# Cross-attention and experts in one kernel: the first blocks' tables in two sub-blocks instead of three, and two values products one chunk later

## The chip, the cores and the metric

The kernel runs on one core of a Trainium2 chip. The metric is the device time of one execution in microseconds (us); three runs of the kernel before gave 897.76, 898.35 and 902.75, median 898.35. The engines have names in the profile: PE is TensorE's matrix multiplication and PEld its weight load, DVE is VectorE, ACT is ScalarE, POOL is GpSimd, and SP is the engine that issues most of the transfers; SPq is its queue.

## The reference

A token matrix x (4 x 1024 tokens of 256 numbers) attends to a context of 77 rows per batch with 16 heads of 64. What comes out is added to x, and each token then goes through two of nine experts (gated feed-forward networks, 256 to 704 and back), whose sum is added again. Cut to what matters:

```
q = layernorm(layernorm(x)) @ Wq;  k, v = split(layernorm(ctx) @ Wkv)      # q scaled and shifted per head
x = x + softmax(q k^T / 8) v @ Wout
logits = layernorm(x) @ Wr;  top 2 of softmax(logits), weights made to sum to 1
x = x + sum over the two experts e:  w_e * ( silu(y Wg[e]) * (y Wu[e]) ) @ Wd[e],   y = layernorm(x)
```

## The kernel before

The keys are folded into the query weights and the output weights into the values, so that attention over a piece of tokens is: scores against a table `g`, a softmax, and a product with a table `u`. The 4096 tokens are eight groups (`NG`) of 512, each of four sub-blocks of 128 tokens: 32 sub-blocks (`N_SUB`). One loop walks over them, and its body holds work of several sub-blocks at different stages. In its step i:

- `scores(i, k)` and `exponentials(i, k)` (lines 271 to 286) for three banks k: TensorE makes 16 x 77 scores, VectorE the maxima of the rows, ScalarE the exponentials;
- `attention_weights(i - 1)` (lines 306 to 313): VectorE normalises into a single buffer `an`;
- `weights_turn(i - 1)` (lines 327 to 335): VectorE transposes in 32 x 32 pieces into a single buffer `anT`; SP writes it to DRAM (`a_d`, 640 KB) and reads it back turned, in four transfers, into `aT` (two buffers). The next transpose must wait until `a_d` is written, the four reads too;
- `values(d)` with d = i - 3 (line 344): TensorE multiplies `aT` by `u`; `attended(d)` (lines 352, 353) adds the product to x and to the router's logits;
- pieces of the routing of groups whose attention is done: `residual` writes x to the output (line 861), `normalised` makes the layer norm y and writes it to `y_d` (line 896), `choices` picks the two experts (lines 903 to 938), `places` gives each token its place in its experts' lists and scatters eight columns of entries there with GpSimd's indirect transfers (line 965). In `choices`, GpSimd makes the token numbers of the entries (lines 932 and 937), and VectorE then writes the weights beside them (line 938). A list of pending work that a generator yields is advanced by `advance(what, n)`: n operations, or all of them.

The experts' work is cut into blocks of 256 or 128 tokens of one expert. Which expert and where its list starts is computed on the chip. For the first six blocks (`EARLY`) this is done when only the first four groups are routed: `early_blocks` is a chain of 20 small VectorE operations after a count by TensorE (lines 984 to 1050). It begins in step 24 of the loop and is advanced by a fixed number of operations in each step. When the chain has ended, `fetch(in_parts=True)` issues for blocks 0 and 1 the list and token gathers on GpSimd's queue (line 1208) and makes generators for the weights, kept in `partly`. From the next step on one part of them is issued per step on SP's queue, behind that step's `a_d` and `aT`: the gate weights (line 1191, 704 KB), the up weights (lines 1193 to 1195, 704 KB in three transfers), the down weights (lines 1197 and 1201, 704 KB in two); a fourth step ends the generator. What is left is issued after the loop. `fetch` stands in the loop's body ahead of the first part of `choices` of the same step.

SP's queue is worked in order: a transfer that waits holds up those behind it. The same holds for each engine's instructions, in the order in which the program writes them; `manual_schedule` leaves that order as written.

After the loop come the blocks. `hidden_pair(j, also)` makes the six chunks of a block's hidden layer (gate and up products, line 1265, then line 1271 on ScalarE and 1272 on VectorE). After each chunk `pump()` advances the pending routing work by up to twelve operations; a yielded `PRODUCT` makes it pause for three chunks (`HOLD`). Then the functions in `also[chunk]` are called. In block 0 these are the values of the last two sub-blocks, whose weights have not come back from DRAM when the loop ends, and the transposition of block 1's tokens, `turn(1)` (line 1251):

```
in_first = {0: [lambda: late_values(N_SUB - 2)], 3: [last_values], 4: [lambda: turn(1)]}
```

`late_values(i)` is `values(i)` and `attended(i)` with the statistics of the sub-block before. `last_values` does this for sub-block 31 and puts the last group's routing and the tables of the later blocks on the list of pending work.

Of the kernel before, what the change touches and what calls it, by code (L numbers as in the profile page):

```python
# [21 lines left out]
def kernel(  # L22
# [222 lines left out]
    def query(i):  # L245

        g, s = divmod(i, NS)
        o, r, _ = zscale[g]
        nc.scalar.activation(
            zs[i % 2][:, : D - 1], xg[g][:, s, : D - 1], AF.Identity,  # L250
            bias=o[:, s : s + 1], scale=r[:, s : s + 1],
        )

    def query_turn(i):
        z = zs[i % 2]
        pz = mm_tile(f"pz{i}")
        for c in range(C):
            nc.tensor.transpose(pz[:, c * P : (c + 1) * P], z[:, c * P : (c + 1) * P], ident)
        zT = zTs[i] = pools["qpool"].tile([P, C, P], F32, tag="zT", name=f"zT{i}")
        nc.scalar.copy(zT.rearrange("p c t -> p (c t)"), pz[:, : C * P])  # L260

    def scores(i, k):

        zT = zTs[i]
        h, n = banks[k]
        if k == 0:
            nmx[i] = stat.tile([P, H], F32, tag="mx", name=f"mx{i}")
        psc = pscs[k] = ps_sc.tile([P, TB], F32, tag=f"sc{k}", name=f"psc{i}_{k}")
        w = n * J + (E if h + n == H else 0)
        for c in range(C):  # L270
            nc.tensor.matmul(  # L271
                psc[:, :w], zT[:, c, :], g_sb[i // NS // GPB][:, c, h * J : h * J + w],
                start=(c == 0), stop=(c == C - 1),
            )
        nc.vector.tensor_reduce(  # L275
            nmx[i][:, h : h + n], psc[:, : n * J].rearrange("p (h j) -> p h j", h=n), AX.X,
            ALU.max, negate=True,
        )

    def exponentials(i, k):  # L280
        h, n = banks[k]
        if k == 0:
            exs[i] = pools["qpool"].tile([P, H, J], F32, tag="ex", name=f"ex{i}")
            sms[i] = stat.tile([P, H], F32, tag="sm", name=f"sm{i}")
        for q in range(n):
            nc.scalar.activation(  # L286
                exs[i][:, h + q, :], pscs[k][:, q * J : (q + 1) * J], AF.Exp,
                bias=nmx[i][:, h + q : h + q + 1], accum_out=sms[i][:, h + q : h + q + 1],
            )
# [12 lines left out]
    def attention_weights(i):  # L302

        ex, sm = exs.pop(i), sms.pop(i)
        rs = stat.tile([P, H], F32, tag="rs", name=f"rs{i}")
        nc.vector.reciprocal(rs, sm)
        an = an_of[0]
        nc.vector.tensor_tensor(  # L308
            an[:, : H * JA].rearrange("p (h j) -> p h j", h=H), ex[:, :, 0:JA],
            rs.unsqueeze(2).to_broadcast([P, H, JA]), ALU.mult,  # L310
        )
        four = H // N2
        nc.vector.tensor_tensor(
            an[:, H * JA :].rearrange("p (m w n) -> p n m w", w=W, n=N2)[:, :, :, :JR],
            ex[:, :, JA:J].rearrange("p (n m) j -> p n m j", n=N2),
            rs.rearrange("p (n m) -> p n m", n=N2).unsqueeze(3).to_broadcast([P, N2, four, JR]),
            ALU.mult,
        )
# [4 lines left out]
    def weights_turn(i):  # L323


        turned = pools["qpool"].tile([P, NQ, Q, KC], F32, tag="anT", name=f"anT{i}", bufs=1)
        nc.vector.transpose(  # L327
            turned.rearrange("p q t k -> p q k t"), an_of[0].rearrange("p (k q t) -> p q k t", q=NQ, t=Q)
        )
        aT = aTs[i] = pools["qpool"].tile([P, NQ, Q * KC], F32, tag="aT", name=f"aT{i}")  # L330
        there = a_d[i % 2]
        nc.sync.dma_start(out=there, in_=turned.rearrange("p q t k -> p (q t k)"))
        by_key = there.rearrange("(a i) (q m) -> q i a m", i=Q, q=NQ)
        for q in range(NQ):
            nc.sync.dma_start(out=aT[q * Q : (q + 1) * Q], in_=by_key[q])
# [28 lines left out]
    with ExitStack() as kvs:  # L364
# [418 lines left out]
        def fill(*what, new=mm_tile):  # L783

            for b, n in what:
                first_keys(b, n, new)
# [96 lines left out]
    def exponential(g):  # L883
        nc.scalar.activation(routed[g]["pb"], routed[g]["pb"], AF.Exp)
# [239 lines left out]
    def of(tiles, j):  # L1124

        return tiles[j % len(tiles)] if j < NBLK else late[id(tiles)]
# [100 lines left out]
    def turned_tile(j):  # L1227
        xT = xTs[j] = late["xT"] if j >= NBLK else pools["spool"].tile(
            [P, C, TS], F32, tag="xT", name=f"xT{j}"
        )  # L1230
        return xT
# [13 lines left out]
    def turn(j):  # L1245

        nh, xT = blocks[j][0], turned_tile(j)
        px = ps_sc.tile([P, TB], F32, tag="sc0", name=f"px{j}").rearrange("p (c t) -> p c t", c=C)
        for c in range(C):
            for h in range(nh):  # L1250
                nc.tensor.transpose(
                    px[:, c, h * P : (h + 1) * P], of(yins, j)[:, h, c * P : (c + 1) * P], ident
                )
        nc.scalar.copy(xT[:, :, : nh * P], px[:, :, : nh * P])  # L1254
# [178 lines left out]
    def advance(what, n=None):  # L1433

        for _ in range(n) if n is not None else iter(int, 1):
            if next(what, None) is None:
                return True
        return False
# [16 lines left out]
    N_SUB = NG * NS  # L1455
    LAG = 3
    chosen, early = None, None
    for i in range(N_SUB + 1):
        g, s = divmod(i, NS)
        now_on = i < N_SUB  # L1460
        d = i - LAG

        gr, sr = divmod(i - LAG + 1, NS)
        q = gr - 1

        if now_on:
            if 0 < i < N_SUB - 1:
                query(i + 1)
            if i:
                scores(i, 0)  # L1470
                fill(*left.get((i, 0), ()))
                exponentials(i, 0)
        if i > 1:
            attention_weights(i - 1)
        if now_on and i:
            scores(i, 1)
            fill(*left.get((i, 1), ()))
            exponentials(i, 1)
        if i > 1:
            weights_turn(i - 1)  # L1480
        if now_on:
            if i:
                scores(i, 2)
                fill(*left.get((i, 2), ()))
            if i == B - 1:
                vsides.close()
            if 0 < i < N_SUB - 1:
                query_turn(i + 1)
            if i:
                exponentials(i, 2)  # L1490
                queries_logits(i)
        else:
            turn(0)
        if d > 0:
            residual_stats(d - 1)
        if gr >= 0 and sr == 1 and q > 0:
            ranks(q - 1)
        if i - LAG + 1 == (G_EARLY + 1) * NS + 2:
            early = early_blocks()
            advance(early, 2)  # L1500
        if d >= 0:
            values(d)

        if s == 0 and 0 < g and g + 1 < NG:
            query_scale(g + 1)
        if s == 1 and g + 2 < NG:
            load_x(g + 2)
        if s == 3 and g + 2 < NG:
            for k in range(NS):
                query_stats(g + 2, k)  # L1510
        if gr >= 0 and sr == 0 and q > 0:
            advance(chosen)
        if gr >= 0 and sr == 1:
            if g + 2 < NG:
                query_variance(g + 2)
            if q >= 0:
                advance(residual(q))
                root(q)
            if g + 2 < NG:
                query_root(g + 2)  # L1520
            nc.scalar.activation(junk, eps_t, AF.Exp)
            if q > 0:
                advance(places(q - 1))
        if gr >= 0 and sr == 2 and q >= 0:
            advance(logits(q))
            exponential(q)
            advance(normalised(q))
        if early is not None:
            if advance(early, 9):
                early = None  # L1530
                now[0] = -1
                fetch(in_parts=True)
        elif partly and advance(partly[0], 1):
            partly.pop(0)
        if gr >= 0 and sr == 3 and q >= 0:
            chosen = choices(q)
            advance(chosen, 14)
        if d >= 0:
            attended(d)
        if i == BH * GPB * NS + LAG - 1:  # L1540
            halves[0].close()
            open_experts()
# [7 lines left out]
    def late_values(i):  # L1550
        residual_stats(i - 1)
        values(i)
        attended(i)
# [6 lines left out]
        rest.append(late_blocks())  # L1560

    rest.append(listed_second_last())
    in_first = {0: [lambda: late_values(N_SUB - 2)], 3: [last_values], 4: [lambda: turn(1)]}


    LAST = NBLK - 1
# [86 lines left out]
```

## Time and profile before

| | |
|---|---|
| median of three runs | 898.35 us |
| the profiled execution | 902.66 us |
| its span, first to last instruction | 900.6 us |
| TensorE busy | 869.1 us, 97% of the span |
| VectorE / ScalarE / GpSimd busy | 592.2 / 356.2 / 312.5 us |
| mean granted TensorE clock | 0.992 |
| attention's loop ends, block 0 begins | about 365 us |

A row of the list in order of time has the start in us from the span's start, the duration, the engine, the line, the operation with what it writes and reads, and how many instructions are merged; in brackets stands how long the engine was idle before, and what ended the idle time. A row of a table by stretches has for PE, PEld, DVE, ACT and POOL the busy time and the number of instructions, then the granted TensorE clock, the busy share of the DMA engines, and what they moved in GB/s. "x20" at line 344 is the ten products of a sub-block, each of which is recorded as two.

### The profile page before, as it was taken

How to read it: one execution, taken by the hardware profiler on the slowest of the kernel's cores; microseconds unless marked ns; L12 is line 12 of the kernel's file. 1: busy time of each engine (PE TensorE's matmuls, PEld its weight loads, DVE VectorE, ACT ScalarE, POOL GpSimd, SP SyncE). 2: the span in 40 equal slices, each digit the busy share in tenths (PEclk: the TensorE clock that was granted, in tenths of full speed). 3: DMA queues.
4: the chain of work that ended last, by engine and by line, in shares of the span. 5: the costliest groups of instructions: out<-in, count | busy, mean ns of one | idle time of the engine just before them, and what ended most of it. 6: DMA issues, size and time to landing. Idle time of an engine off the chain costs nothing. (4 is left out here: it accounts for less than half of the span.)

```text
span 900.6 us, 13822 instructions
## 1 busy us (share of the span) xinstructions
PE 869.1 (97%) x3864; PEld 677.8 (75%) x3864; DVE 592.2 (66%) x1806; ACT 356.2 (40%) x1500; POOL 312.5 (35%) x325
## 2 busy tenths in 40 slices
PE   8999999998999998899999999999999999999996
PEld 6545787866787776788787777777777777778885
DVE  4857788778999978443826666666666656665641
ACT  3668687858788685241121111111111111111110
POOL 3000000404233430537256435435445435445232
PEclk9999999999999999899999999999999999999998
DMA  6116556566766676899579779779779778789722
GB/s 222 49 67 202 152 187 193 113 182 149 216 176 191 188 210 203 213 298 185 158 226 298 218 220 315 223 217 311 224 221 317 219 217 218 226 230 322 217 33 24
DMA packets 132956, 181.18 MB, mean 201 GB/s; under 512 B 26951, under 2 KB 98127, under 8 KB 132752
## 3 DMA queue, kind: packets, MB, share of 16 engines
q1 hardware_dynamic: 115322, 162.90, 60.5%
q0 software_dynamic: 17344, 17.26, 10.3%
q8 instruction: 31, 0.51, 0.3%
q14 instruction: 45, 0.37, 0.1%
q10 hardware_dynamic: 214, 0.13, 0.0%
HBM read 141.54 MB, written 40.39 MB: 202 GB/s over the span
## 5 line engine op out<-in xcount | busy, mean ns | idle before, releaser
L1265 PE MATMUL pg<-xT,wgu 128*128 128x256 f32 x1144 | 253.0, 380 | 3.0 <-DVEq L1606 1.5
L1265 PEld LDWEIGHTS pg<-xT,wgu 128*128 128x128 f32 x1144 | 215.5, 190 | 33.0 <-ACT xT L1254 2.5
L286 ACT ACTIVATE ex<-psc,mx 128x77 f32<-128x77 f32 x512 | 158.7, 331 | 70.3 <-DVE mx L275 66.6
L1343 PE MATMUL po<-wd,hid 128*128 128x256 f32 (+1 forms) x804 | 180.9, 380 | 0.0
L1343 PEld LDWEIGHTS po<-wd,hid 128*128 128x128 f32 (+1 forms) x804 | 149.2, 187 | 28.1 <-issue 3.7
L344 PE MATMUL po<-u,aT 128*128 128x265 f32 x640 | 159.2, 405 | 8.8 <-DMA aT<-a_d 8.8
L344 PEld LDWEIGHTS po<-u,aT 128*128 128x128 f32 x640 | 150.4, 313 | 11.6 <-issue 9.9
L1378 POOL DMA_INDIRECT out_dram<-co,ids x63 | 100.2, 1591 | 167.7 <-DVE co L1346 139.4
L965 POOL DMA_INDIRECT list_d<-r_entry,r_pli x64 | 66.8, 1043 | 260.9 <-DVE r_pli L963 148.1
L1238 DVE STREAM_TRANSPOSE xT<-yin 32x128 f32<-32x128 f32 (+1 forms) x544 | 148.4, 273 | 12.5 <-DMA yin<-y_d,ids 3.7
L271 PE MATMUL psc<-g,zT 128*128 128x462 f32 (+1 forms) x384 | 141.5, 514 | 2.6 <-ACT zT L260 2.6
L1271 ACT ACTIVATE sl<-pg 128x256 f32<-128x256 f32 x130 | 49.7, 384 | 233.8 <-PE pg L1265 162.1
L1272 DVE TENSOR_TENSOR hid<-pg,sl 128x256 f32<-128x256 f32 x130 | 55.0, 424 | 128.9 <-ACT sl L1271 94.7
L271 PEld LDWEIGHTS psc<-g,zT 128*128 128x128 f32 x384 | 71.7, 190 | 61.0 <-issue 46.0
L286 ACT ACTIVATION_READ_ACCUMULATOR ex<-psc,mx 128x1 f32 x512 | 107.9, 211 | 0.0
L327 DVE STREAM_TRANSPOSE anT<-an 128x1280 f32<-128x1280 f32 x32 | 79.6, 2486 | 14.3 <-DMA a_d<-anT 13.8
L1208 POOL DMA_INDIRECT yin<-y_d,ids x67 | 70.5, 1053 | 27.0 <-issue 25.5
L275 DVE TENSOR_REDUCE mx<-psc 128x6 f32<-128x462 f32 (+1 forms) x96 | 53.5, 558 | 18.8 <-PE psc L271 17.7
L1346 DVE TENSOR_SCALAR co<-po,ids 128x256 f32<-128x256 f32 x67 | 32.2, 483 | 48.4 <-PE po L1343 46.8
L308 DVE TENSOR_TENSOR an<-ex,rs 128x1024 f32<-128x1024 f32 x32 | 39.2, 1225 | 1.1
L1331 ACT COPY hid<-ph 128x384 f32<-128x384 f32 x15 | 7.2, 479 | 78.4 <-PE ph L1326 78.4
L1307 ACT ACTIVATE hs<-psg 128x512 f32<-128x512 f32 x15 | 9.0, 597 | 65.3 <-issue 42.2
(311 smaller groups left out, 762.5 us busy)
## 6 DMA issues: line engine op xcount, KB each, us to landing
wgu<-in_L_ffn_Wg_dram SPq DMA_DIRECT2D x41, 704.0 KB
wd<-in_L_ffn_Wd_dram SPq DMA_DIRECT2D x41, 640.0 KB
wgu<-in_L_ffn_Wu_dram SPq DMA_DIRECT2D x41, 512.0 KB
a_d<-anT SPq DMA_DIRECT2D x32, 640.0 KB
aT<-a_d SPq DMA_DIRECT2D x128, 160.0 KB
wgu<-in_L_ffn_Wu_dram SPq DMA_DIRECT2D x41, 128.0 KB
x<-in_x_dram SPq DMA_DIRECT2D x8, 512.0 KB
out_dram<-x SPq DMA_DIRECT2D x8, 512.0 KB
```

What stands on the lines that cost most here:

```text
L271: nc.tensor.matmul(psc[:, :w], zT[:, c, :], g_sb[i // NS // GPB][:, c, h * J : h * J + w], start=(c == 0), stop=(c == C - 1),)
L275: nc.vector.tensor_reduce(nmx[i][:, h : h + n], psc[:, : n * J].rearrange("p (h j) -> p h j", h=n), AX.X, ALU.max, negate=True,)
L286: nc.scalar.activation(exs[i][:, h + q, :], pscs[k][:, q * J : (q + 1) * J], AF.Exp, bias=nmx[i][:, h + q : h + q + 1], accum_out=sms[i][: ...
L327: nc.vector.transpose(turned.rearrange("p q t k -> p q k t"), an_of[0].rearrange("p (k q t) -> p q k t", q=NQ, t=Q))
L344: nc.tensor.matmul(po[:, :DE], aT[:, :, n], u_sb[b][:, n, :], start=(n == 0), stop=(n == KC - 1))
L965: i = nc.gpsimd.indirect_dma_start(out=list_d[:, :], out_offset=bass.IndirectOffsetOnAxis(ap=place_i[:, s : s + 1], axis=0), in_=entries[k ...
L1208: return nc.gpsimd.indirect_dma_start(out=dst, out_offset=None, in_=src, in_offset=bass.IndirectOffsetOnAxis(ap=offsets, axis=0), **kw,)
L1238: yield nc.vector.transpose(xT[q : q + Q].rearrange("p c (h t) -> p h c t", t=P)[:, :nh, :, a : a + Q], of(yins, j)[a : a + Q].rearrange(" ...
L1265: nc.tensor.matmul(pg[:, g, :], w[:, c, at : at + P], xT[:, c, :], start=(c == 0), stop=(c == C - 1),)
L1272: nc.vector.tensor_tensor(hid[:, f, :], pg[:, 1, :], sl, ALU.mult)
L1343: nc.tensor.matmul(po[rows, :D], hid[:, f, at], d[:, f, :], start=(f == 0), stop=(f == NF))
L1378: i = nc.gpsimd.indirect_dma_start(out=out_r, out_offset=bass.IndirectOffsetOnAxis(ap=rows_of(j, h, rows), axis=0), in_=cos[j][:, h, :], i ...
```

## The change

Two lines change. The chain of the first six blocks' tables is advanced by 14 operations per step instead of 9, so that it ends in step 25 instead of step 26, and `fetch` is called one step earlier. And in block 0 the values of sub-block 30 are called after chunk 1 instead of chunk 0, those of sub-block 31 after chunk 4 instead of chunk 3; `turn(1)` stays after chunk 4, behind them.

```diff
         if early is not None:
-            if advance(early, 9):
+            if advance(early, 14):
                 early = None
                 now[0] = -1
                 fetch(in_parts=True)
         elif partly and advance(partly[0], 1):
             partly.pop(0)
...
     rest.append(listed_second_last())
-    in_first = {0: [lambda: late_values(N_SUB - 2)], 3: [last_values], 4: [lambda: turn(1)]}
+    in_first = {1: [lambda: late_values(N_SUB - 2)], 4: [last_values, lambda: turn(1)]}
```

The functions that these lines call are unchanged:

```
    def late_values(i):
        residual_stats(i - 1)
        values(i)
        attended(i)

    def last_values():
        late_values(N_SUB - 1)
        residual_stats(N_SUB - 1)
        rest.append(routing(NG - 1))
        rest.append(late_blocks())
```

The steps in which the weights of blocks 0 and 1 are issued on SP's queue:

| step | before | after |
|---|---|---|
| 26 | | gate 0 |
| 27 | gate 0 | up 0 |
| 28 | up 0 | down 0 |
| 29 | down 0 | |
| 30 | | gate 1 |
| 31 | gate 1 | up 1 |
| 32 | up 1 | down 1 |
| after the loop | down 1 | |

## The prediction

> **What bounds the kernel now.** I began with the page's busy row and the group of the values product (line 344), went to TensorE's list of instructions in order of time for the end of attention, and from its releaser to the SP queue.
>
> ```profile
> PE 869.1 (97%) x3864; PEld 677.8 (75%) x3864; DVE 592.2 (66%) x1806; ACT 356.2 (40%) x1500; POOL 312.5 (35%) x325
> ...
> L344 PE MATMUL po<-u,aT 128*128 128x265 f32 x640 | 159.2, 405 | 8.8 <-DMA aT<-a_d 8.8
> ```
>
> TensorE is the bound: 869.1 of 900.6 us. All that TensorE waits for `aT`, the transposed weights that return through DRAM, is 8.8 us, five waits, and 6.2 us of them are three waits between 349 and 380 us:
>
> ```profile
> 349.74 4.94 PE L344 MATMUL po<-u,aT 128*128 128x265 f32 x20 [0.32 <-DMA aT<-a_d]
> 354.51 0.60 PE L1251 MATMUL px<-ident,yin 128*128 128x128 f32 x4
> 358.69 6.56 PE L344 MATMUL po<-u,aT 128*128 128x265 f32 x20 [3.57 <-DMA aT<-a_d]
> 365.08 1.89 PE L1265 MATMUL pg<-xT,wgu 128*128 128x256 f32 x8
> 366.81 4.86 PE L344 MATMUL po<-u,aT 128*128 128x265 f32 x20
> 371.50 5.34 PE L1265 MATMUL pg<-xT,wgu 128*128 128x256 f32 x24
> 379.16 6.56 PE L344 MATMUL po<-u,aT 128*128 128x265 f32 x20 [2.31 <-DMA aT<-a_d]
> 385.56 1.89 PE L1265 MATMUL pg<-xT,wgu 128*128 128x256 f32 x8
> 387.28 0.60 PE L1251 MATMUL px<-ident,yin 128*128 128x128 f32 x4
> ```
>
> The four L344 rows are the values of sub-blocks 28, 29, 30, 31. A values product takes 4.86 us, but 6.56 after the two long waits: each wait costs its idle time and 1.70 more. From 387.28 us on TensorE runs the experts with no wait for DMA, so what is won or lost before this row is what the kernel wins or loses. The most that can be had here is 3.57 + 2.31 + 0.32 + 2 x 1.70 = 9.6 us.
>
> What `aT` waits for is read from the SP queue (every row is the issue of transfers, in queue order):
>
> ```profile
> 345.37 0.40 SPq L1197 DMA_DIRECT2D wd<-in_L_ffn_Wd_dram  x1
> ...
> 346.63 0.51 SPq L332 DMA_DIRECT2D a_d<-anT  x1
> 353.59 1.74 SPq L335 DMA_DIRECT2D aT<-a_d  x4
> 356.11 0.34 SPq L332 DMA_DIRECT2D a_d<-anT  x1
> 359.89 1.73 SPq L335 DMA_DIRECT2D aT<-a_d  x4
> 361.66 0.43 SPq L861 DMA_DIRECT2D out_dram<-x  x1
> 362.90 0.41 SPq L1191 DMA_DIRECT2D wgu<-in_L_ffn_Wg_dram  x1
> 363.41 0.68 SPq L332 DMA_DIRECT2D a_d<-anT  x1
> 374.08 1.74 SPq L335 DMA_DIRECT2D aT<-a_d  x4
> ```
>
> The loads of `aT` go out when the write of `a_d` has landed. With no weights ahead a write lands in 359.89 - 356.11 = 3.8 us; with an expert's down weights (704 KB) ahead in 353.59 - 346.63 = 7.0; with the output and the gate weights ahead in 374.08 - 363.41 = 10.7. From the issue of `aT` to TensorE's start are 5.1 us (353.59 to 358.69, and 374.08 to 379.16). So the wait of 3.57 us belongs to the down weights ahead of a_d(29), and the wait of 2.31 to what lies ahead of a_d(31).
>
> **Part one: the tables in fewer sub-blocks.** The same 20 small VectorE operations are spread as 14 + 6 instead of 9 + 9 + 2. Nothing is removed. The five that go into sub-block 24 take 0.95 us there (L1011 to L1025, 297.42 to 298.37) and are missing in 25, so `early_ai`, for which GpSimd's gathers wait, is made at the same time (299.0). What moves is `fetch`, one sub-block ahead, and with it every weight load of blocks 0 and 1 on the SP queue: gate weights 0 from sub-block 27 to 26, up 28 to 27, down 29 to 28; gate weights 1 from 31 to 30, up 32 to 31, down from after the loop into 32. I follow the landing of each `a_d` (before in brackets; the row "with the same load ahead" is the measure):
>
> - a_d(26) now has 704 KB ahead: about 321.3 (319.12). Its `aT` is used at 330.94: hidden, and it costs as long as that cover stands nothing.
> - a_d(27): output, up weights, GpSimd's scatters, as many bytes as before, 12.7 us after the one before it as then: 334.0 (331.80).
> - a_d(28): y and down weights instead of y and up weights: 11.5 later, 345.5 (343.35). Its `aT` then comes at 350.6 instead of 349.74; TensorE waits about 1 us there.
> - a_d(29): nothing ahead, but VectorE's transpose waits for a_d(28) and ends at 348.0, plus 3.8: 351.8 (353.59). `aT` at 356.9: the wait of 3.57 becomes about 1.
> - a_d(30): gate weights 1 ahead; about 360.7 (359.89). `aT` some 6 us later, 366.8.
> - a_d(31): output and up weights ahead, where output and gate weights were: the same bytes, the same scatters, 14.2 us after the one before it: 374.7 after taking off 0.2 for scatters begun earlier (374.08).
>
> So the late loads are only passed along: what a_d(29) gains, a_d(31) doesn't keep.
>
> A second step of this part is on GpSimd's queue. `fetch` is called before `choices(4)` instead of after it, so the eight gathers stand ahead of the copies of line 937, and VectorE's line 938 waits for those copies:
>
> ```profile
> 293.73 0.34 POOL L937 COPY r_entry<-r_tg 128x4 int32<-128x4 int32 x2
> ...
> 309.93 0.97 POOL L1208 DMA_INDIRECT ids<-list_d,early_ai  x1 [0.30 <-issue]
> ```
> ```profile
> 309.71 0.42 DVE L938 TENSOR_TENSOR r_entry<-r_m,r_rb 128x4 f32<-128x4 f32 x2
> ```
>
> The gathers end at 310.9, and 0.22 + 0.34 + 0.3 us of small operations bring the copies to 311.5; VectorE would come to line 938 at 310.06 and stands 1.5 us. Behind it are the residual and the row maxima of sub-block 27, and ScalarE's exponentials wait for those. VectorE has 3.2 us idle ahead of 329.19, which takes the stall up; until there TensorE loses 0.4 to 1.0 us on `zT`. This is ahead of the waits above and is swallowed by them as long as the DMA chain sets their ends. I take 0 on the end, with 1.0 us as the price if the cover is gone.
>
> **Part two: values one chunk later.** Sub-block 30's values move from behind chunk 0 to behind chunk 1, 31's from behind chunk 3 to behind chunk 4. No instruction is added or removed. Values 30 are not late today, so that move pays only where part one makes them late: TensorE would be at them at about 363.3 + 1 and waits to 366.8. Values 31 are different: TensorE now waits at 379.16 with chunk 4 still to do (1.72 us, 385.56 to 387.28). Afterwards chunk 4 lies ahead of the wait. The routing of the last group stays where it is, since it is held until the first chunk of block 1 by the product of the second-last group.
>
> The sum has thus one term that counts: gain = 1.72 - d, where d is the delay of a_d(31). With d = 374.7 - 374.08 = 0.6 the turn at 387.28 comes at 386.2: 1.1 us gained. All later work keeps its order. The profiled execution, 902.66 us with a span of 900.6, becomes 901.6; the median of the runs shown, 898.35, lies 4.3 below the profiled execution, and I take the same 1.1 from it: **897.2**.
>
> **A rule against the trace.** The Trainium skill (TensorE: Matmul & The Clock Gate, section on HAM oscillation) says that idle gaps of TensorE matter to its clock above some 3.4 us. By that the new wait of about 3 us ahead of values 31 would leave the clock alone. The trace differs:
>
> ```profile
> 376.00:380.00 4.00, 1.69 (x7) 1.26 (x7) 1.32 (x5) 0.38 (x1) 2.92 (x5) 1.00 1.10 274
> 380.00:384.00 4.00, 4.00 (x12) 3.23 (x12) 0.00 (x0) 0.00 (x0) 0.43 (x1) 0.57 0.92 276
> ```
>
> After 2.31 us idle the granted clock (third number from the end) fell to 0.57 for 3.4 us, worth the 1.70. By the rule the gain would be 1.1 + 1.7 = 2.8 us; I keep the row, 1.1, and both for the range.
>
> **Rivals.**
> - *The DMA chain catches up.* If the 704 KB ahead of a_d(26) are drained while that queue idles (SP shows no write in flight from 319 to 324), nothing is passed along: a_d(28) at 343.3, a_d(29) at 349.5, a_d(30) at 358.8, a_d(31) about 13 later, 371.8. Then the end of values 31 is 381.7 to 383.5: up to 5.6 us gained, 892.8 to 894.6. For it speaks the idle DMA before each landing, against it that a_d(27) and a_d(28) today take 12.7 and 11.5 us each with these bytes.
> - *Nothing is seen.* d is as large as chunk 4: 898.4. The tables' part alone would do that if TensorE's 1 us on `zT` also stays.
> - *Slower, through VectorE's wait at line 938.* If it delays the transposes of sub-blocks 27 to 31 by its 1.5 us each without recovery, a_d(31), 0.6 late already, is up to 5 us late when the up weights' three issues on SP (334.21 to 336.18: 2 us where the gate weights take 0.4) also stand ahead of it. It decides from d = 1.72 on. Price: 2 to 3.5 us, 900.4 to 902.
>
> **Chances.** The forecast (896 to 898.2) 0.48; catching up 0.20; nothing 0.18; slower 0.14. I count changes under 0.5% (4.5 us), about what a measurement of this kernel can tell, as same. Half of the catching up is over 4.5 us gained, with a little for the rule on the clock: faster 0.12. Most of the slower case stays below 4.5 us, but the delay may pass into the experts: slower 0.10. Same 0.78. The range takes in the catching up nearly whole and the slower case to 3 us: 893.2 to 901.4; the forecast's own is 895.5 to 898.9.
>
> **What would show it.** In the changed profile: the wait of values 29 falls from 3.57 to about 1; a new wait ahead of values 30; a longer one, about 3 us, ahead of values 31, with a slow clock after it; the turn at 387.28 at 386.2; VectorE idle about 1.5 us ahead of line 938 with GpSimd as releaser; a_d(26) landing some 2 us later. The prediction is wrong if a_d(31) lands well before 374, if TensorE has a new wait in the experts, or if sub-blocks 26 to 28 get longer.

## The result and the profile after

The changed kernel is slower, by less than half a per cent: median 900.86 us of 20 runs (897.94 to 904.99) against 898.06 of 20 runs of the kernel before (893.27 to 904.10), ratio 1.0044 with a 95% interval of 1.0028 to 1.0059, or some 3.9 us by the ratio. A second comparison (further down) gave 1.0023, 1.0005 to 1.0041. The time lies in the predicted range (893.2 to 901.4), but the sign is wrong: 1.1 us gained was forecast.

Single executions of one kernel lie up to 11 us apart (line 984, ahead of which nothing was changed, begins anywhere from 277.0 to 284.0 us in the profiles here), and the two profiled ones happen to be a slow one of before (902.66) and a fast one of after (898.0). They can't be compared by their spans. What can be compared is the stretch from the count for the tables (line 984 on TensorE: 283.64 us before, 280.69 after) to the turn of block 1's tokens (line 1251: 387.28 and 384.63), since everything that the change touches lies between the two. It takes 103.6 us before and 103.9 after, so this pair of profiles shows hardly any of the 3.9 us; a second pair further down shows 3.2. From that turn to the end are 513.3 us in the first profile of before, which has a lone wait of 1.3 us for `xT` at 437 us, and 511.4 or 511.5 in all thirteen other profiles here, of whatever version: nothing is passed on into the experts.

The page of the changed kernel, the rows of the values product, the scores and VectorE's transpose:

```profile
L344 PE MATMUL po<-u,aT 128*128 128x265 f32 x640 | 157.6, 402 | 4.4 <-DMA aT<-a_d 4.2
...
L271 PE MATMUL psc<-g,zT 128*128 128x462 f32 (+1 forms) x384 | 142.2, 515 | 7.4 <-ACT zT L260 4.6
...
L327 DVE STREAM_TRANSPOSE anT<-an 128x1280 f32<-128x1280 f32 x32 | 79.4, 2483 | 19.4 <-DMA a_d<-anT 19.3
```

TensorE waits less for `aT` ahead of the values (4.2 us, 8.8 before) and more ahead of the scores (7.4, 2.6 before); VectorE's transposes wait longer for `a_d` to be written (19.3, 13.8 before). Some of the waiting has moved from the values into the loop. Where, is seen in TensorE's list in order of time:

```profile
344.67 3.37 PE L271 MATMUL psc<-g,zT 128*128 128x462 f32 x8 [1.09 <-ACT zT L260]
348.59 1.34 PE L271 MATMUL psc<-g,zT 128*128 128x317 f32 x4 [0.55 <-ACT lg L297]
...
350.13 4.94 PE L344 MATMUL po<-u,aT 128*128 128x265 f32 x20
354.91 0.60 PE L1251 MATMUL px<-ident,yin 128*128 128x128 f32 x4
357.05 4.94 PE L344 MATMUL po<-u,aT 128*128 128x265 f32 x20 [1.54 <-DMA aT<-a_d]
361.82 3.62 PE L1265 MATMUL pg<-xT,wgu 128*128 128x256 f32 x16
367.95 6.55 PE L344 MATMUL po<-u,aT 128*128 128x265 f32 x20 [2.52 <-DMA aT<-a_d]
374.34 5.34 PE L1265 MATMUL pg<-xT,wgu 128*128 128x256 f32 x24
379.86 4.93 PE L344 MATMUL po<-u,aT 128*128 128x265 f32 x20 [0.18 <-issue]
384.63 0.60 PE L1251 MATMUL px<-ident,yin 128*128 128x128 f32 x4
```

The wait of values 29 is down from 3.57 to 1.54 us and without the slow clock, as forecast. A new one of 2.52 stands ahead of values 30, with 1.7 us of slow clock. Values 31 hardly wait: TensorE comes to them at 379.7 us, just when their `aT` is due (374.61, below, plus 5.1). They begin 99.2 us after line 984, 95.5 before: 3.65 later, less chunk 4 (1.72) and less the slow clock that is gone there (1.63), leaves 0.3 us lost. SP's queue says why:

```profile
312.35 0.43 SPq L1191 DMA_DIRECT2D wgu<-in_L_ffn_Wg_dram  x1
313.21 0.34 SPq L332 DMA_DIRECT2D a_d<-anT  x1
319.88 3.47 SPq L335 DMA_DIRECT2D aT<-a_d  x4
...
346.77 0.34 SPq L332 DMA_DIRECT2D a_d<-anT  x1
350.67 1.73 SPq L335 DMA_DIRECT2D aT<-a_d  x4
353.21 0.41 SPq L1191 DMA_DIRECT2D wgu<-in_L_ffn_Wg_dram  x1
355.07 0.34 SPq L332 DMA_DIRECT2D a_d<-anT  x1
361.69 1.75 SPq L335 DMA_DIRECT2D aT<-a_d  x4
...
366.09 0.41 SPq L332 DMA_DIRECT2D a_d<-anT  x1
374.61 1.76 SPq L335 DMA_DIRECT2D aT<-a_d  x4
```

The two writes that now have gate weights ahead, a_d(26) and a_d(30), take 6.7 and 6.6 us from issue to landing; a_d(29), which has no weights ahead any more, takes 3.9. Counted from line 984, a_d(30) lands at 81.0 (76.3 before) and a_d(31) at 93.9 (90.4).

The late writes are felt in the loop too. VectorE's transpose of sub-block 28, before and then after:

```profile
332.87 2.50 DVE L327 STREAM_TRANSPOSE anT<-an 128x1280 f32<-128x1280 f32 x1
```
```profile
333.01 2.46 DVE L327 STREAM_TRANSPOSE anT<-an 128x1280 f32<-128x1280 f32 x1 [4.48 <-DMA a_d<-anT]
```

It waits 4.48 us for a_d(27), where it had no wait. VectorE's next reduction of scores (line 275), for which ScalarE's exponentials wait, stands behind it and comes 3.1 us later, counted from line 984.

### The profile page after: what moved, and what is told of

It is laid out like the page before. It is cut to its first block, busy times and chain, and to the rows that moved or that the text cites. A ratio compares the mean times of both kernels' runs of the same rounds, so it can differ in the third digit from the quotient of the medians.

```text
span 896.1 us, 13820 instructions
## 1 busy us (share of the span) xinstructions
PE 866.4 (97%) x3864; PEld 676.3 (75%) x3864; DVE 591.0 (66%) x1806; ACT 356.1 (40%) x1500; POOL 311.6 (35%) x325
## 5 line engine op out<-in xcount | busy, mean ns | idle before, releaser
L327 DVE STREAM_TRANSPOSE anT<-an 128x1280 f32<-128x1280 f32 x32 | 79.4, 2483 | 19.4 <-DMA a_d<-anT 19.3
```

The source lines that it names most:

```text
L327: nc.vector.transpose(turned.rearrange("p q t k -> p q k t"), an_of[0].rearrange("p (k q t) -> p q k t", q=NQ, t=Q))
```

## The experiments

Three theories stood against each other. A: the weights that go out one step earlier delay the chain of `a_d` writes. B: VectorE waits at line 938 for GpSimd's copies behind the gathers. C: the values' move costs. The first four kernels were meant to take the change apart. Each ratio is to the kernel before in the same comparison.

**The tables alone.** The line of the values is put back:

```diff
-    in_first = {1: [lambda: late_values(N_SUB - 2)], 4: [last_values, lambda: turn(1)]}
+    in_first = {0: [lambda: late_values(N_SUB - 2)], 3: [last_values], 4: [lambda: turn(1)]}
```

> Only the tables' half of the change (14 operations per step, fetch one step earlier); the values stay behind chunks 0 and 3. Theory A (the loads of blocks 0 and 1, one step earlier on the SP queue, delay the chain of a_d writes; the values' move only takes chunk 4 out of the way): slower than before by more than the whole change, by about 1.7 us more, so +4 to +6 us; in its trace a_d(31) lands about 3.5 us later, counted from the count of the tables on TensorE (line 984), than in the kernel before. Theory B (VectorE's wait for the token numbers behind the gathers): the same sign, +1.5 to +4. Theory C (the values' move is what costs): no difference, -1 to +1.

Measured: ratio 1.0058 (1.0037 to 1.0078), +5.2 us: more than the whole change, as A says, though the intervals overlap. a_d(31) lands 93.1 us after line 984, 2.6 later than in the first profile of before where 3.5 were expected; values 30 wait 5.61 us.

**The values alone.** The kernel before with the second changed line only.

> Only the values' half (behind chunks 1 and 4); the tables as before. Theory A: faster by chunk 4's 1.7 us, and by up to 1.7 us more where the shorter wait ahead of values 31 spares the slow clock: -1.7 to -3.4 us. Theory B: the same. Theory C: slower by the whole 3 to 4 us.

Measured: 0.9979 (0.9966 to 0.9992), -1.9 us. The move of the values is a gain, as A and B said, and C falls. In its trace values 31 follow chunk 4 with no wait at all.

**The gathers behind the choices' first part.** To put GpSimd's copies ahead of the gathers again, `fetch` is called after the choices of its step:

```diff
                 now[0] = -1
-                fetch(in_parts=True)
+                fetch_due = True
...
             advance(chosen, 14)
+        if fetch_due:
+            fetch_due = False
+            fetch(in_parts=True)
```

> The whole change, but fetch is called after the choices of its step, so that GpSimd's copies of the token numbers stand ahead of the gathers as in the kernel before; SP's queue as in the whole change. Theory A: as slow as the whole change, within 1 us (+2 to +5 against before). Theory B: the loss is gone (-2 to +1), and VectorE's wait at line 938 with it. Theory C: as slow as the whole change.

Measured: 1.0024 (1.0006 to 1.0042), +2.2 us. But this kernel does not do what it was meant to. The first 14 operations of `choices` end before the copies, which are issued in the next step, so the copies still stand behind the gathers. Its last gather and its copies:

```profile
306.85 0.95 POOL L1208 DMA_INDIRECT ids<-list_d,early_ai  x1 [0.30 <-issue]
...
308.15 0.32 POOL L937 COPY r_entry<-r_tg 128x4 int32<-128x4 int32 x2
```

Its time therefore says nothing on B; it is in effect a third measurement of the whole change. The traces do tell. GpSimd and VectorE in the whole change, in order of time:

```profile
308.26 0.32 POOL L937 COPY r_entry<-r_tg 128x4 int32<-128x4 int32 x2
```
```profile
306.90 0.17 DVE L930 TENSOR_TENSOR seen<-r_cums,r_sel 128x9 f32<-128x9 f32 x1
307.11 0.40 DVE L938 TENSOR_TENSOR r_entry<-r_m,r_rb 128x4 f32<-128x4 f32 x2
```

VectorE's line 938 ran at 307.11, before the copies had even begun (308.26). It doesn't wait for them; that they write other columns of the tile may be why. The wait that I had costed at 1.5 us does not exist.

**The weights held back one step.** After `fetch` one step is left empty, so that SP's queue has the order of the kernel before:

```diff
                 fetch(in_parts=True)
+                hold = 1
+        elif partly and hold:
+            hold -= 1
         elif partly and advance(partly[0], 1):
```

> The whole change, but the first part of the weights is held back one step, so that SP's queue has the order of the kernel before; GpSimd's and VectorE's order as in the whole change. Theory A: the loss is gone, and the values' move gains its 1.7 us: -3.4 to 0 against before. Theory B: still slower, +1.5 to +4. Theory C: as slow as the whole change.

Measured: 0.9968 (0.9954 to 0.9983), -2.9 us. With the weights in their old steps the loss is gone, though the gathers still stand ahead of GpSimd's copies as in the changed kernel. That settles A against B.

**Which load?** The next two split the early weights: block 0's early and block 1's as before (an empty step after the last part of block 0: `hold = 1` at the `pop`), and the other way round (block 0 held one step, block 1's first part sent at the `pop`).

> The whole change, but only block 0's weights go out one step earlier; the first part of block 1 stays in step 31 as before (one empty step between). Theory A1 (the loss starts with the gate weights in step 26 and is passed along): still slower, +1 to +4 us against before. Theory A2 (the late landing of a_d(26) to a_d(28) is made good in step 29, which has no load any more, and only gate weights 1 in step 30 delay the last two writes): faster, -5 to -2 us; a_d(30) and a_d(31) land no later after line 984 than in the kernel before (76.3 and 90.4 us).

> The whole change, but block 0's weights stay in steps 27 to 29 as before and only block 1's go out one step earlier (30 to 32). Theory A1: as fast as the values' move alone, -3 to -1 us. Theory A2: the loss is here, +1 to +5 us; four steps in a row with loads, a_d(30) lands 3 us or more later after line 984 than before, and a_d(31) with it.

Measured: block 0 early 1.0019 (1.0004 to 1.0035), +1.7 us; block 1 early 1.0053 (1.0037 to 1.0069), +4.7 us. The greater loss is with block 1's gate weights in step 30, as A2 says, though a_d(30) and a_d(31) land there only 2.8 and 1.1 us later than in the first profile of before, less than A2 expected; and A2's -5 to -2 for block 0 early was missed. Against the values' move alone (-1.9), block 0 early still costs 3.6 us. Its writes 30 and 31 land at 77.5 and 90.5, 1.2 us later than before and as before (76.3 and 90.4), so that part of A2 held for the last write. What differs inside the loop is that VectorE's transpose of sub-block 28 waits 4.84 us for a_d(27) (0.62 in the values' move alone). Its waits of TensorE from 330 to 390 us (in all, how many, the longest):

```profile
PE po L344 <- DMA aT<-a_d: 3.2, 2, 1.9
PE psc L271 <- DVE r_o L916: 1.5, 1, 1.5
PE psc L271 <- ACT zT L260: 1.1, 1, 1.1
PE psc L271 <- ACT lg L297: 0.8, 1, 0.8
```

The last three, 3.4 us, are ahead of the scores; they stand in this stretch of the whole change too (1.1, 1.1 and 0.6), and of the values' move alone they do not. That they come from the late transpose is read from the order of the rows; no run takes it apart. The two costs don't add: 3.6 and 6.6 make 10.2, and the whole change costs 5.8 more than the values' move alone, 4.0 by the second comparison. Why is not shown.

**Fewer loads in the loop.** If the load on the queue is the cause, taking more of it away must gain. First all of block 1's weights go after the loop (parts are advanced in the loop only while two blocks are pending), block 0's staying in steps 27 to 29. Then block 0's down weights too, which are used only after block 1's hidden layer:

```diff
-        elif partly and advance(partly[0], 1):
-            partly.pop(0)
+                hold = 1
+        elif partly and hold:
+            hold -= 1
+        elif partly and issued < 2:
+            issued += 1
+            advance(partly[0], 1)
...
+    advance(partly[1], 2)
     for parts in partly:
         advance(parts)
```

> Weights of block 0 as in the kernel before (steps 27 to 29), all of block 1's after the loop, values moved. By theory A a_d(31) has 704 KB less ahead and lands 2 to 3 us earlier than before (87 to 88 us after line 984); the wait of values 29 stays (2 to 4 us and the slow clock). -5 to -3 us against before, unless block 1 then waits for its weights.

> As the one before, and also block 0's down weights, which are needed only after block 1's hidden layer, go out after the loop, behind block 1's gate and up weights. By theory A values 29 no longer wait behind the down weights: -8 to -4 us against before. If the rule of this stretch were not the load on the queue but VectorE's and ScalarE's own chain, no better than -3.

Measured: block 1 late 0.9973 (0.9954 to 0.9991), -2.4 us: a_d(31) lands 86.4 us after line 984, 4 sooner than before, but this is no better than the weights held (0.9968), so the expected -5 to -3 was missed. Values 31 had no wait left to lose there; values 29 still wait 3.05 us behind the down weights. With those after the loop as well: 0.9942 (0.9920 to 0.9963), **-5.2 us**, median 887.77 of only 7 runs against 893.04. It beats the kernel before, and by that the changed one. TensorE and SP in that version, in order of time:

```profile
353.70 4.86 PE L344 MATMUL po<-u,aT 128*128 128x265 f32 x20
358.39 3.62 PE L1265 MATMUL pg<-xT,wgu 128*128 128x256 f32 x16
361.85 4.75 PE L344 MATMUL po<-u,aT 128*128 128x265 f32 x20
366.44 5.34 PE L1265 MATMUL pg<-xT,wgu 128*128 128x256 f32 x24
372.71 4.93 PE L344 MATMUL po<-u,aT 128*128 128x265 f32 x20 [0.93 <-DVE hid L1272]
377.48 0.60 PE L1251 MATMUL px<-ident,yin 128*128 128x128 f32 x4
```
```profile
352.60 0.34 SPq L332 DMA_DIRECT2D a_d<-anT  x1
355.59 1.74 SPq L335 DMA_DIRECT2D aT<-a_d  x4
357.38 0.43 SPq L861 DMA_DIRECT2D out_dram<-x  x1
359.52 0.34 SPq L332 DMA_DIRECT2D a_d<-anT  x1
365.43 1.74 SPq L335 DMA_DIRECT2D aT<-a_d  x4
```

No wait for `aT` is left; a_d(30) lands in 3.0 us and a_d(31), with only the output ahead, in 5.9. The stretch takes 94.2 us.

**The pair again, and two controls.** The kernel before and the changed kernel once more, for second profiles.

> The kernel before, for a second profile. In the first one 103.64 us lie between the count on TensorE (line 984) and the turn of block 1 (line 1251), and 513.3 us behind it, where every other profile has 511.4 or 511.5. If the first profile was an unlucky execution, this one has about 101 us (the values' move alone has 99.1, and is 1.9 us faster) and 511.4. If not, 103 to 104.

> The whole change, for a second profile. If the stretch between line 984 and the turn of block 1 carries the whole difference of the medians, it has about 104 to 105 us here, 3 to 4 more than the kernel before, and 511.4 us follow it. +3 to +5 us against before.

Measured: before 1.0006 (0.9993 to 1.0019), changed 1.0023 (1.0005 to 1.0041), +2.1 us, a little under what was expected. The stretch takes 103.4 us before and 106.6 after, so this pair shows +3.2. Whether the first profile of before was unlucky in this stretch stays open: 103.4 where 101 was expected speaks against it, but this second profiled execution (898.04) is the slowest of its twenty runs (median 895.62), and the tables held, below, whose queue and values are in the order of before, takes 101.3 in an execution under its median. Block 0 early and block 1 early take 101.3 and 102.0, though their medians lie above that of before. So the sizes of the losses here rest on the times of many runs; a single profile shows where a landing or a wait moved, not by how much the kernel did. What followed the turn in the first profile was unlucky: it is 511.4 here. The later landing of the last write is plainer than in the first pair, 95.7 against 90.1, and so is the wait ahead of values 30 in the changed kernel:

```profile
371.25 6.27 PE L344 MATMUL po<-u,aT 128*128 128x265 f32 x20 [4.26 <-DMA aT<-a_d]
```

Then the fastest version with the values at their old places, and the tables' half with the weights held.

> Down weights of block 0 and all of block 1 after the loop, as in the fastest version so far, but the values of sub-blocks 30 and 31 behind chunks 0 and 3 as in the kernel before. If the values' move pays only where the weights come back late, it is worth nothing here: -6 to -4 us against before, as with the move. If it pays its chunk of 1.7 us anyway: -4 to -2.5.

> Only the tables' half (14 operations per step, gathers ahead of the copies), with the weights held so that SP's queue is as before; values as before. By theory A this does nothing: -1 to +1 us, against +5.2 for the tables' half with the weights one step earlier. If the tables' spread or GpSimd's order costs by itself: +1.5 to +4.

Measured: 0.9961 (0.9948 to 0.9974), -3.5 us, and 1.0015 (0.9992 to 1.0039), +1.3 us. In the first the values' move seems worth its chunk even where `aT` comes back early (-5.2 with it), but the intervals overlap. The second can't be told from no change, nor from the 1.5 us or more of the other theory; the same tables with the weights one step earlier cost 5.2. The weights held (0.9968), which has this spread of the tables too, is no slower than the values' move alone (0.9979), which has not: these runs show no cost of the spread by itself.

The landings over all profiles, in us after line 984 (SP's queue, issue of the `aT` loads):

| | a_d(26) | a_d(30) | a_d(31) |
|---|---|---|---|
| gate 0 in step 26: changed kernel twice, tables alone, gathers behind choices, block 0 early | 38.6 to 39.7 | | |
| gate 0 in step 27: before twice, values alone, held, block 1 early, block 1 late, down 0 late and its old values, tables held | 34.8 to 36.2 | | |
| gate 1 in step 30: changed kernel twice, tables alone, gathers behind choices, block 1 early | | 79.1 to 83.2 | 91.6 to 95.7 |
| gate 1 in step 31: before twice, values alone, held, block 0 early, tables held | | 74.1 to 77.5 | 87.4 to 90.5 |
| block 1 after the loop: three versions | | 72.3 to 74.8 | 82.1 to 86.4 |

Whether a write has the gate weights ahead of it separates the groups: a_d(26), (30) and (31) land at least 2.4, 1.6 and 1.1 us later with them one step earlier. From issue to landing a_d(26) and a_d(30) take 6.0 to 8.2 us in the versions of the first and the third row. All versions send the weights on the same queue as `a_d`, so the runs do not tell whether the order of the queue delays the write or the DMA engines that both share.

## Why the prediction was right or wrong

- *The frame was right in outline only.* The loss is made ahead of block 1's turn, by late landings of `a_d`, and chunk 4 moved ahead of values 31 is a gain (the values alone: -1.9 us). But the sum had one term, the delay d of a_d(31), with a break-even at 1.72 us, and that is too little: block 0 early loses 3.6 us against the values' move alone with a_d(31) only 1.2 us later than there.
- *The delay d was mis-sized*, and this is the step that failed: 0.6 us in the sum, 3.5 and 5.6 in the two pairs. The intervals from a_d(26) to (29) were right: 12.7, 11.5 and 6.3 forecast, 13.1, 11.3 and 6.4 measured. Wrong were the two writes that got 704 KB of gate weights ahead. a_d(26) was given 5.2 us from issue to landing (316.12 to 321.3), and a_d(30) 4.6 if it is issued at 356.11 as before, while the row shown for a write behind one load of this size said 7.0. They took 6.7 and 6.6. From a_d(29) to a_d(30) were 11.0 us where 8.9 were forecast. The last interval was off the other way, 12.9 for 14.0.
- *What the delay did* was different too. The sum let a_d(31) set the end. In the first pair it is a_d(30), 4.7 us later than before where 0.8 was forecast: the new wait ahead of values 30 with its slow clock costs 4.2 us, and TensorE is as late at values 31 as their `aT`.
- *"What a_d(29) gains, a_d(31) doesn't keep"* was right, but too mild.
- *The waits.* About 1 us ahead of values 29 was right (1.54). Ahead of values 28 about 1 us was forecast and none came. Ahead of values 30 the prediction's figures (364.3 and 366.8) give 2.5 us, and 2.52 and 4.26 were measured; the slow clock there was not counted. The wait of 3 us ahead of values 31 didn't come.
- *TensorE's loss in the loop* was taken as 0.4 to 1.0 us and swallowed. It was 2.8 us in steps 30 and 31 of the first pair (1.14 + 1.09 + 0.55), and its cause is another: as far as the order of the rows shows, VectorE's transposes, which wait for the late writes. The prediction named longer sub-blocks 26 to 28 as a sign of being wrong, and this sign came.
- *VectorE's wait at line 938* was wrong: it ran before the copies.
- *The rivals.* "Slower" came true with its break-even, d over 1.72 us, and near its price (2 to 3.5 us for the measured 3.9 and 2.1), but not by its mechanism; that the number fits is luck. "The DMA chain catches up" fell: counted from line 984, a_d(26) to (28) land 3.7 to 4.1 us later than before, a_d(29), without a load ahead, lands as before, and a_d(30) is late again.
- *The base.* The gain was taken from a median of three runs next to a profile 4.3 us above it, of which 1.9 us lay in the experts. The median of 20 runs came out at 898.06, so this did not decide the sign.

## What to carry to other kernels

Where a write, its read-back and bulk loads share one queue, price a load by the row of a write that already stands behind such a load, and ask for every load which of the next writes it goes ahead of; sending weights "earlier" can mean ahead of the one transfer that the next stage waits for. Here weights sent later, after the last `aT`, gained 3.5 us, and 5.2 with the values' move, and no expert block waited for them. And a wait that is inferred from the order of two engines' instructions, as that of line 938 was, stays a guess until a trace shows the one engine idle. So it is with an experiment's edit: only its trace shows whether the order that it was to change has changed.

## What the runs showed of the hardware

Three stretches of the changed kernel around the wait of 2.52 us ahead of values 30 (busy times of PE, PEld, DVE, ACT and POOL, then the granted clock, the DMA share and GB/s):

```profile
364.00:368.00 4.00, 1.48 (x8) 1.01 (x6) 1.54 (x9) 2.78 (x6) 3.09 (x4) 1.00 0.94 250
368.00:372.00 4.00, 4.00 (x10) 3.24 (x11) 2.50 (x13) 1.36 (x3) 1.87 (x2) 0.57 1.09 336
372.00:376.00 4.00, 4.00 (x20) 3.79 (x19) 2.92 (x17) 0.00 (x0) 1.37 (x4) 1.00 0.42 117
```

The granted clock falls to 0.57 for one stretch and is back in the next. The 0.57 is a mean: in stretches of 1 us or less after the 2.31 us of the kernel before, the clock is 1.00 until 380 us, 0.50 from 381 to 383.5, and between the two (0.72 and 0.64) in the stretches at both ends. It is at half for about 3.4 us, which is what the prediction's "0.57 for 3.4 us" comes to, and costs 4 x 0.43 = 1.7 us.

How long must TensorE be idle for that? Between 280 and 400 us the values products after ten waits of 1.25 to 1.88 us took 4.93 to 4.96 us, and those after thirteen waits of 1.95 to 5.61 us took 6.27 to 7.46. That looks like a sharp border, but it is none: earlier in the same traces two waits of 2.38 us ended differently, in the kernel before and in the values' move alone:

```profile
207.97 0.44 PE L258 MATMUL pz<-ident,z 128*128 128x128 f32 x2 [2.38 <-ACT z L249]
208.25 4.85 PE L344 MATMUL po<-u,aT 128*128 128x265 f32 x20
```
```profile
245.36 0.44 PE L258 MATMUL pz<-ident,z 128*128 128x128 f32 x2 [2.38 <-ACT z L249]
245.63 6.49 PE L344 MATMUL po<-u,aT 128*128 128x265 f32 x20
```

The granted clock is 1.00 after the first and falls to 0.50 after the second. Over the fourteen profiles, the first 25 us left out, no wait of TensorE from 1.0 to 1.76 us lowered the clock and all from 2.52 us on did. Of ten between 1.81 and 2.38 us six did (1.81, 1.95, 2.23, 2.31, 2.33, 2.38) and four did not (1.88, 2.05, 2.08, 2.38); what decides between them is not shown. The prediction weighed a rule by which idle gaps matter above some 3.4 us (the Trainium skill, TensorE: Matmul & The Clock Gate, section on HAM oscillation): by it the wait of 2.52 us would have cost 2.5 us, and it cost 4.2; the measurement decides. So here a wait of up to 1.76 us costs only itself, and one of 2.52 us or more, ahead of a values product, 1.3 to 2.6 us on top.
